# Layer 0 of a two-layer kernel: where the group sums, the spread of the values and the scalings of the last inverse stand

## The chip, the cores and the metric

The kernel runs on one core of one Trainium2 chip. The core has five engines that run side by side, [...]: TensorE (PE in the profile, its weight loads PEld), VectorE (DVE), ScalarE (ACT), GpSimd (POOL) and SyncE (SP), which here only issues DMAs. The metric is the device time of one whole execution in microseconds (us); lower is better. All data is float32.

## The reference, cut to what matters

The input is x, 4 batches of 32 images of 128 x 128 (in the code B = 4, T = 32, and an image's rows and columns are H = C = 128). Layer 0 is a Fourier attention block:

```python
xn = inorm(gn(x))                            # group norm, then per-image norm
k, q, v = (fno(xn, w, s) for w, s in ...)    # spectral convolutions, 32 heads
p = softmax(einsum('bntk,bnsk->bnts', q, k)) # 32 x 32 per head and batch
a = inorm(fno(einsum('bnts,bnsk->bntk', p, v)) + gn(x))
m = inorm1(spectral1(gelu(inorm0(spectral0(inorm(a))) + skip))) ...
x = x + inorm(m) + a
```

Spectral convolutions are products of the low Fourier modes (64 x 33 per image) with weights, so the kernel computes with modes: forward transforms as matmuls with cosines and sines, products in mode space, inverse transforms as matmuls again. Layer 1 (an attention over 1024 tokens per row block and a mixture of experts) follows and takes what layer 0 wrote; it is not changed.

## The kernel before, in words

`layer0` runs over the four batches b. A batch has these stages:

- **The products with the values** (`for x0 in range(0, KX, NK)`, L936 on): modes of the images are broadcast from DRAM into `xb` (L941, four buffers), copied into PSUM as `xw` (L950), multiplied with the value weights `gb` into `u`, most of them on VectorE (L963) and some on GpSimd (L959), and contracted on TensorE with the attention probabilities `pr` into `po` (L898, helper `product`).
- **Inverse transform, the statistics, the spectrum and gelu** (`inverse`, `stats`, `spectra`, `inverse_of`, `gelu`).
- **The boundary to the next batch**, which overlaps the end of batch b with the attention of batch b + 1: `image_scales` (group norm of the next batch), `spectra(1, ...)` (second spectrum of this batch), `spectra_of_images` (modes of the next batch), `coefficients` (the factors c2, c3, cq of the last normalisation), `attention_weights` (scores, softmax, probabilities through DRAM as `prd` and `pr`), and the last inverse of this batch, `back`, which adds its result into `xr` and stores it.

Most of layer 0 is placed by a scheduler that works with estimated times; `behind(later, earlier)` forces an order without a wait. The order that results is fixed in the program. Each engine then takes its queue in order: an instruction that waits holds everything behind it.

Places that the change touches:

- `image_scales` (L438): VectorE makes `both`, TensorE sums it over the partitions (`bg`, L380, in `sums`), and VectorE copies it to `by_group` (L448), all ahead of `colg` and `sv`. `by_group` is read only much later, in `turn` (L914).
- `value_weights` (L604): VectorE makes the weights `g`, one row per head and quarter of the modes. Two DMAs write them to DRAM as `gd` (L620), four DMAs read them back into `gb` (L625), each repeating 16 heads' rows over 8 groups of partitions. It runs once, ahead of batch 0.
- `attention_weights` (L637): `pa` and `pb` (L675, L677), the score matmuls `sp` and `sp0` (L690, L692), `spt` and `spt0` (L695, L700), `sc` (L705 to L715), `mx`, `less`, the exponential `ex` (L722), `sm`, and `ph` (L732, two halves on GpSimd). Its three hooks put work of batch b between: the scalings `g` (L1283, 32 ACT instructions: 16 ahead of `spt`, 8 ahead of `ex`, 8 after it) and GpSimd's additions into x (L1293, four).
- `back` (L359 `four`, L343 `y` in `row_products`, L357 copies `v`) with `last` (L1331): four VectorE instructions per group, each scaling one image by its c3 and adding it. `skip_matrix` (L764 `cm`, L768 `cd`, L769 `cp`) makes the skip weights of the next batch.
- PSUM tags: `wide` has two buffers, shared by `xp`, `y`, `xw` and the sums; `a` and `b` have two each. In SBUF the tag `v` has three.

Of the kernel before, what the change touches and what calls it, by code (L numbers as in the profile page):

```python
# [7 lines left out]
F32 = mybir.dt.float32  # L8
# [122 lines left out]
def layer0(  # L131
# [201 lines left out]

    def row_products(spec, a, ahead=()):


        wide = [ps.tile([P, 2, 512], F32, name="y1", tag="wide") for _ in range(2)]
        for slot in range(4):
            c = slice(slot * P, slot * P + P)
            for k, trig in enumerate((cos_back, sin_back)):  # L340
                for g in range(4):
                    r = slice(32 * g, 32 * g + 32)
                    mm = nc.tensor.matmul(  # L343
                        wide[g // 2][:, g % 2, c],
                        spec[r, 4 * a + slot, 64 - 64 * k : 192 - 64 * k],
                        trig[r],
                        start=k == 0,
                        stop=k == 1,
                    )
                    for earlier in ahead:  # L350
                        behind(mm, earlier)
        return wide
# [7 lines left out]

    def back(spec, a, take, ahead=(), copy=None, apart=False):

        wide = row_products(spec, a, ahead)
        for g in range(4):
            four, inverted, _ = four_images(
                wide,
                g,
                copy or evacuate,
                dict(tag="pr", bufs=6) if apart and a else dict(tag="v", bufs=3),
                "a" if apart and g % 2 else "b",  # L370
            )
            take([image(a, g, k) for k in range(4)], four)
        return inverted
# [64 lines left out]
    def image_scales(sv, gm, gv, shift):  # L438

        gr, _ = inv_std("gn_r", gv, 1)  # L440
        gs = one("gs")
        nc.vector.tensor_mul(gs, gm, gr)

        both = small.tile([P, 2, 32], F32, name="both", tag="both")
        nc.vector.tensor_scalar(both[:, 0], of_group, gr, None, ALU.mult)
        nc.vector.tensor_scalar(both[:, 1], of_group, gs, -1.0, ALU.mult, ALU.mult)
        by_group = small.tile([P, 2, 32], F32, name="by_group", tag="by_group")
        nc.vector.tensor_copy(by_group, sums("bg", ones, both, "a"))  # L448
        colg = small.tile([P, NX], F32, name="colg", tag="colg")
        nc.vector.tensor_scalar(colg, cols, gr, None, ALU.mult)  # L450
        gs128 = one("gs128")
        nc.vector.tensor_scalar(gs128, gs, 128.0, None, ALU.mult)
        gg = one("gg")
        nc.vector.tensor_mul(gg, gs, gs128)
        gr2 = one("gr2")
        nc.vector.tensor_mul(gr2, gr, gr)
        grs = one("grs")
        nc.vector.tensor_scalar(grs, gs, gr, -2.0, ALU.mult, ALU.mult)
        nc.vector.tensor_scalar(sv[:, 1], sv[:, 1], gr2, gg, ALU.mult, ALU.add)
        nc.vector.scalar_tensor_tensor(sv[:, 1], sv[:, 0], grs, sv[:, 1], ALU.mult, ALU.add)  # L460
        nc.vector.tensor_scalar(sv[:, 0], sv[:, 0], gr, gs128, ALU.mult, ALU.subtract)
        sv_op = nc.vector.tensor_scalar(sv, sv, 1.0 / NPIX, None, ALU.mult)
        return by_group, colg, shift, sv, sv_op

# [16 lines left out]
    def spectra_of_images(b, xt, normed, then=None):  # L481


        _, colg, shift, sv, _ = normed
        n = 1 + KY
# [96 lines left out]
        for g in GROUPS:  # L582
            z = grp.tile([P, GI, 2, 32], F32, name="z", tag="z")
            made = half_rows([xt[:, g + t] for t in range(GI)], z, z32[:, :, g : g + GI])
            if g == 0:
                ysc, scaled = image_weights(sv, made)
            if g == GI and then is not None:
                then(made)
# [8 lines left out]
        unfold(1)  # L597
        return xx, (xe, xm), xd, edges, ysc

    def value_weights():  # L600
# [8 lines left out]
        behind(nc.vector.tensor_scalar(p1, pw[:, :, :KA, 0], hv[:, 3:4], None, ALU.add), normed[4])  # L609
        gd = dram.tile([2, NH, NM], F32, name="gd")  # L610
        for ri, (b, d, op) in enumerate(
            ((v_re, v_im, ALU.subtract), (v_im, v_re, ALU.add))
        ):
            g = prep.tile([P, KX // 4, KY], F32, name=f"g{ri}")
            behind(nc.vector.tensor_scalar(g, pw[:, :, :, ri], hv[:, 2:3], None, ALU.mult), normed[4])
# [3 lines left out]
            nc.vector.tensor_tensor(g[:, :, :KA], g[:, :, :KA], t1, ALU.add)  # L619
            written = nc.sync.dma_start(  # L620
                out=gd[ri].rearrange("n (q m) -> (n q) m", q=4), in_=g.rearrange("p x y -> p (x y)")
            )
        for ri in range(2):
            for k in range(2):
                read = nc.sync.dma_start(  # L625
                    out=gb[:, k, ri],
                    in_=gd[ri, 16 * k : 16 * k + 16].unsqueeze(0).to_broadcast([8, 16, NM]),
                )
                if ri == 0:
                    behind(read, written)  # L630

# [3 lines left out]
    def attention_weights(b, front, hooks=None):  # L635

        xx, (xe, xm), _, (x32, w32), _ = front  # L637
        xs = per_image("xs")
# [57 lines left out]
        if ahead is not None:  # L696
            behind(act, ahead)
        ahead = hooks[1](act) if hooks else None
        spt0 = small.tile([2 * NH, T], F32, name="spt0", tag="ym")
# [14 lines left out]
        for o, i in halves:  # L714
            nc.tensor.matmul(o[:, :, 0], both_plus[: 2 * NH], spt0[:, i], start=False, stop=True)  # L715

        mx = small.tile([2 * NH, half], F32, name="mx", tag="mx")
        nc.vector.tensor_reduce(mx, sc, AX.X, ALU.max)
        less = grp.tile(nn, F32, name="less", tag="v", bufs=3)
        nc.vector.tensor_tensor(less, sc, mx.unsqueeze(2).to_broadcast(nn), ALU.subtract)  # L720
        ex = grp.tile([2 * NH, half, 2, T], F32, name="ex", tag="pr", bufs=6)
        softmax = nc.scalar.activation(ex, less.unsqueeze(2).to_broadcast([2 * NH, half, 2, T]), AF.Exp)  # L722
        if ahead is not None:
            behind(softmax, ahead[0])
        sm = small.tile([2 * NH, half], F32, name="sm", tag="mx")
# [3 lines left out]
        for h in range(2):  # L729
            r = slice(32 * h, 32 * h + 32)  # L730
            first = ex.rearrange("n t r d -> n (t r d)")[r, T - half * h :]
            product = nc.gpsimd.tensor_tensor(  # L732
                ph[r],
# [3 lines left out]
            )  # L737
            if ahead is not None:
                behind(product, ahead[1])
        if hooks:  # L740
# [58 lines left out]
    front = spectra_of_images(0, loaded, normed)  # L799
    value_weights()  # L800

# [37 lines left out]
    big, late = (p.__enter__() for p in (pools[-1], right[-1]))  # L839
    weights = attention_weights(0, front)  # L840
    bd = skip_matrix(weights[2], front[4])

# [41 lines left out]
    for b in range(B):  # L884
        xt = loaded
        by_group = normed[0]
        xd = front[2]
# [46 lines left out]
        for x0 in range(0, KX, NK):  # L934
# [3 lines left out]
            for i in range(4):  # L938
                xb = late.tile([P, 2, NK * KY], F32, name="xb", tag="xb")[:, :, :m]
                for r in range(2):  # L940
# [5 lines left out]
                        .to_broadcast([8, 16, m]),  # L946
                    )
                xw = ps.tile([P, 2, 512], F32, name="xw", tag="wide")[:, :, :m]
                for r in range(2):
                    c = nc.scalar.copy(xw[:, r], xb[:, r])  # L950
                    if x0 == 0:
                        behind(c, weights[4])
                for k in range(2):
# [99 lines left out]
        def negative(spec, slots):  # L1053

            nc.scalar.activation(spec[:, slots, :64], spec[:, slots, P:], AF.Copy, scale=-1.0)

# [221 lines left out]
        c2, c3, cq = (made[n] for n in ("c2", "c3", "cq"))  # L1278
        negative(spec, slice(0, GI))

# [14 lines left out]
        images_of = [slice(g, g + GI) for g in GROUPS]  # L1295
        if b + 1 < B:
            def first_half(copied, on_pool):

                for t in range(T // 2):
                    act = scale(t)  # L1300
                    behind(act, copied)
                for i in images_of[:2]:
                    behind(add_scaled(i), on_pool)
                return act

            def third_quarter(scores):

                for t in range(T // 2, 3 * T // 4):
                    act = scale(t)
                    behind(act, scores)  # L1310
                return act, add_scaled(images_of[2])

            def rest(softmax, product):

                for t in range(3 * T // 4, T):
                    behind(scale(t), softmax)
                roots["added"] = add_scaled(images_of[3])
                behind(roots["added"], product)

            weights = attention_weights(b + 1, front, (first_half, third_quarter, rest))  # L1320
        else:
# [4 lines left out]
        for a in HALVES:  # L1326
            groups = [slice(16 * a + g, 16 * a + g + GI) for g in (0, GI)]

            def last(images, four):
                for j, t in enumerate(images):  # L1330
                    nc.vector.scalar_tensor_tensor(  # L1331
                        xr[:, t], four[:, j], c3[:, t : t + 1], xr[:, t], ALU.mult, ALU.add
                    )

# [12 lines left out]
            if b + 1 < B:  # L1347
                inverted = back(spec, a, last, weights[1:2] if a == 0 else (), nc.scalar.copy)
            else:
# [646 lines left out]
```

## Time and profile before

| | us |
|---|---|
| median of 3 runs | 2974.37 (2972.92 to 2975.74) |
| the profiled execution | 2975.87 |
| its span in the profile | 2974.2 |
| batch 0 until its first `po` matmul | 88.28 |
| `po` stages of batches 1, 2, 3 begin | 293.02, 498.14 and 702.91 (a period of 205) |
| layer 1's score loop begins | 887.36 |

| engine | busy us | share of the span |
|---|---|---|
| PE | 2741.9 | 92% |
| DVE | 2189.5 | 74% |
| ACT | 2314.2 | 78% |
| POOL | 2031.1 | 68% |

The span runs from the first instruction to the last; the profiled execution's own time lies 1.67 us above it, and 1.50 us above the median of the runs. The shares are means over stages with different limits: layer 1 takes some 2087 us of the span, so the page's totals say little of layer 0. For layer 0 the chain of waits, the timeline of each engine, and the busy time in chosen stretches are read.

### The profile page before, as it was taken

The numbers are of one execution on the slowest core, as the hardware profiler recorded it, in microseconds if no ns is written. First come the engines' busy times: TensorE is split into PE (matmuls) and PEld (weight loads), VectorE is DVE, ScalarE is ACT, GpSimd is POOL, SyncE is SP. The second block draws the span as 40 slices with busy tenths as digits, with TensorE's granted clock in tenths as the row PEclk, the third lists the DMA queues.
The fourth block names the chain that finished last, engine by engine and source line by source line (L and its number), as shares of the span: only waits on it lengthen the run. The fifth ranks groups of instructions, "written<-read, shape, count | busy, mean of one in ns | idle before, by whom it ended". The sixth has DMA issues, their size and how long they took to land.

```text
span 2974.2 us, 52576 instructions
## 1 busy us (share of the span) xinstructions
PE 2741.9 (92%) x19442; PEld 1356.0 (46%) x19442; DVE 2189.5 (74%) x4934; ACT 2314.2 (78%) x3217; POOL 2031.1 (68%) x1801
## 2 busy tenths in 40 slices
PE   7798988988878999999899999999999999999997
PEld 4365564664644443343444343444444443444443
DVE  4876787788766677775678688666778766877877
ACT  2554555456358999899999999989999998999992
POOL 1703605417308897878987878898787889798773
PEclk7899999999989999999999999999999999999998
DMA  5503304205011101002010100111010020100000
GB/s 127 157 1 66 121 1 103 84 7 149 18 51 43 33 1 40 8 11 62 1 26 15 26 15 8 36 29 33 15 26 15 8 58 13 28 12 22 15 15 15
DMA packets 151985, 112.58 MB, mean 38 GB/s; under 512 B 36366, under 2 KB 140081, under 8 KB 151217
## 3 DMA queue, kind: packets, MB, share of 16 engines
q1 hardware_dynamic: 148465, 107.13, 14.1%
q8 instruction: 154, 2.52, 0.4%
q10 hardware_dynamic: 3264, 2.10, 0.2%
q14 instruction: 102, 0.84, 0.1%
HBM read 68.19 MB, written 20.04 MB: 30 GB/s over the span
## 4 chain that ended last, share of the span: by engine, by line
PE 60%; POOL 13%; ACT 11%; DVE 9%; issue 6%; DMA 1%; SPq 0%; POOLq 0%; DVEq 0%; ACTq 0%
PE d L1786 20%; PE po L1805 12%; PE px L1692 6%; ACT r L1836 5%; PE n L1786 4%; POOL e L1845 3%; POOL e L1844 3%; PE po L898 3%; POOL u L959 2%; ACT e L1852 2%; PE pz L305 2%; POOL kx L1451 2%; DVE r L1841 1%; PE px L1093 1%; DVE xc L1696 1%
## 5 line engine op out<-in xcount | busy, mean ns | idle before, releaser
L1841 DVE TENSOR_TENSOR r<-n,r 128x1024 f32<-128x1024 f32 (+1 forms) x1056 | 962.0, 953 | 479.9 <-PE n L1786 397.9
L1844 POOL TENSOR_TENSOR e<-r 128x512 f32<-128x512 f32 x528 | 674.1, 1277 | 270.7 <-DVE r L1841 270.3
L1836 ACT ACTIVATE r<-d 128x1024 f32<-128x1024 f32 (+1 forms) x1056 | 793.3, 803 | 65.3 <-PE n L1786 57.3
L1848 ACT ACTIVATE r<-r 128x1536 f32<-128x1536 f32 x528 | 784.1, 1485 | 16.8
L1845 POOL TENSOR_TENSOR e<-e,r 128x512 f32<-128x512 f32 x528 | 672.0, 1273 | 41.4
L1786 PE MATMUL d<-qe,ke 32*128 32x512 f32 (+3 forms) x2304 | 606.9, 603 | 39.9 <-ACT r L1836 36.0
L1805 PE MATMUL po<-e,kx 128*128 128x512 f32 (+3 forms) x1152 | 594.9, 605 | 16.0 <-POOL e L1857 16.0
L1786 PE MATMUL n<-qe,ke 32*128 32x512 f32 (+3 forms) x2304 | 606.8, 602 | 0.0
L1786 PE MATMUL n<-qf,kf 32*128 32x512 f32 (+3 forms) x2304 | 554.0, 555 | 0.0
L1786 PE MATMUL d<-qf,kf 32*128 32x512 f32 (+3 forms) x2304 | 552.8, 556 | 0.0
L1696 DVE SCALAR_TENSOR_TENSOR xc<-px,wgt,xc 128x128 f32<-128x128 f32 x1024 | 358.3, 350 | 40.8 <-PE px L1692 9.7
L1852 ACT ACTIVATE e<-e 128x512 f32<-128x512 f32 x528 | 326.4, 618 | 67.3 <-POOL e L1845 66.3
L1805 PEld LDWEIGHTS po<-e,kx 128*128 128x128 f32 x1152 | 176.0, 188 | 394.7 <-issue 309.3
L1786 PEld LDWEIGHTS d<-qe,ke 32*128 32x128 f32 x2304 | 176.6, 183 | 359.2 <-ACT r L1836 339.1
L1786 PEld LDWEIGHTS d<-qf,kf 32*128 32x128 f32 x2304 | 220.7, 186 | 176.2 <-issue 163.8
L1692 PE MATMUL px<-we,x2t 128*128 128x512 f32 x512 | 264.3, 602 | 6.4 <-DVE xc L1696 5.3
L959 POOL TENSOR_TENSOR u<-xb,gb 128x858 f32<-128x858 f32 (+1 forms) x112 | 221.3, 2026 | 65.2 <-PE po L898 48.9
L1786 PEld LDWEIGHTS n<-qf,kf 32*128 32x128 f32 x2304 | 228.5, 186 | 19.5 <-issue 11.5
L1110 POOL TENSOR_TENSOR spec<-part,part 128x512 f32<-128x512 f32 x16 | 25.3, 1580 | 305.8 <-DVE part L1107 111.0
L963 DVE TENSOR_TENSOR u<-xw,gb 128x858 f32<-128x858 f32 (+1 forms) x208 | 216.6, 1111 | 17.6 <-ACT xw L950 13.3
L898 PE MATMUL po<-u,pr 128*32 128x429 f32 (+1 forms) x1280 | 149.4, 531 | 40.4 <-POOL u L959 35.8
L1786 PEld LDWEIGHTS n<-qe,ke 32*128 32x128 f32 x2304 | 177.5, 183 | 10.7 <-DVE r L1841 2.2
(417 smaller groups left out, 3365.8 us busy)
## 6 DMA issues: line engine op xcount, KB each, us to landing
xb<-xd SPq DMA_DIRECT2D x128, 214.5 KB
xc<-x SPq DMA_DIRECT2D x29, 512.0 KB
x<-x SPq DMA_DIRECT2D x16, 512.0 KB
qf<-qe SPq DMA_DIRECT2D x64, 128.0 KB
out<-xc SPq DMA_DIRECT2D x15, 512.0 KB
x<-in_x SPq DMA_DIRECT2D x14, 512.0 KB
xb<-xd SPq DMA_DIRECT2D x32, 198.0 KB
gb<-gd SPq DMA_DIRECT2D x4, 1056.0 KB
```

Of the source, the lines that this page charges most:

```text
L898: mm = nc.tensor.matmul(*args, **kw)
L959: weighed = nc.gpsimd.tensor_tensor(u, xb, gk, ALU.mult)
L1692: nc.tensor.matmul(px, x2t[:, k * P : (k + 1) * P], we[:, e0 : e0 + 4], start=True, stop=True)
L1696: nc.vector.scalar_tensor_tensor(xc[:, k], px[:, e], wgt[:, k, e0 + e : e0 + e + 1], xc[:, k], ALU.mult, ALU.add)
L1786: nc.tensor.matmul(o, k, q, start=turn == 0 or g > 0, stop=turn == 1 or g > 0)
L1805: nc.tensor.matmul(sums[c, h][:, q0 : q0 + c1 - c0], kx[:, jb], e[:, c0:c1], start=jb == 0, stop=is_last and q0 > 2 * P, skip_group_check= ...
L1836: nc.scalar.activation(r[:, g], d, AF.Ln, scale=1.0 / DSCALE)
L1841: nc.vector.tensor_tensor(r[:, g], part, r[:, g], ALU.mult)
L1844: nc.gpsimd.tensor_tensor(e, r[:, 1], r[:, 2], ALU.add)
L1845: nc.gpsimd.tensor_tensor(e, e, r[:, 0], ALU.add)
L1848: nc.scalar.activation(r, r, AF.Exp, scale=-1.0)
L1852: nc.scalar.activation(e, e, AF.Exp)
```

## The change

It touches layer 0 alone and has these parts:

1. `both` is made at the end of `image_scales`; its sum `bg` is taken later, among the row transforms of the next images, and ACT copies it to `by_group`. In batch 0 `image_weights` is called at the second group of images.
2. `value_weights` keeps its weights in SBUF. A new function, `spread_values`, repeats the rows over the partitions by matmuls: 16 PSUM tiles of 128 x 528, two matmuls of 128 x 264 each, with a picked identity as weights; ACT copies each tile to `gb`. The six DMAs by way of DRAM are gone.
3. In batches 0 to 2, c3 is gathered per row of `spec` (`of_slot`, `c3s`, on VectorE) and multiplied into `spec` by one GpSimd instruction of 128 x 1024, ahead of the inverse. `last` becomes one addition per group.
4. The scalings: 24 on ACT ahead of `spt`, with the sign flip `negative` after the eighth; the last 8 on VectorE, after the last product of the scores and ahead of `spt0`.
5. The last inverse's first half begins within the attention: half of `y` after the score matmuls, half after `sc`; the first copy `v` stands ahead of `ex`, the other copies right behind it.
6. `ph` is split: its first half on GpSimd, its second on VectorE.
7. The first load of `xb` of the second and later column blocks is ordered behind the read of `pr`; in batches 1 to 3 the first `xw` copies are ordered behind the last copy `v`.

```diff
-    def row_products(spec, a, ahead=()):
+    def row_products(spec, a, ahead=(), slots=range(4), wide=None):
...
-    def back(spec, a, take, ahead=(), copy=None, apart=False):
-        wide = row_products(spec, a, ahead)
+    def back(spec, a, take, begun=(), copy=None, apart=False):
+        wide, *ready = begun or [row_products(spec, a)]
         for g in range(4):
-            four, inverted, _ = four_images(
...
+            four, inverted, roots["v"] = (
+                ready[g] if g < len(ready) else four_images(
...
-        by_group = small.tile([P, 2, 32], F32, name="by_group", tag="by_group")
-        nc.vector.tensor_copy(by_group, sums("bg", ones, both, "a"))
...
-            if g == 0:
+            if g == (GI if b == 0 else 0):
                 ysc, scaled = image_weights(sv, made)
+            if g == 2 * GI:
+                groups = sums("bg", ones, both, "a")
+                behind(summing["bg"], made)
+                nc.scalar.copy(by_group, groups)
...
-            g = prep.tile([P, KX // 4, KY], F32, name=f"g{ri}")
+            g = grp.tile([P, KX // 4, KY], F32, name=f"g{ri}", tag="v", bufs=3)
...
-            written = nc.sync.dma_start(
-                out=gd[ri].rearrange("n (q m) -> (n q) m", q=4), in_=g.rearrange("p x y -> p (x y)")
...
+    def spread_values(of_row):
+        n = KX * KY // 8
+        picked = grp.tile([P, 2, 4, 8, 16], F32, name="picked", tag="z")
+        for k in range(2):
+            nc.scalar.copy(picked[:, k], steps(ident[:, 64 * k :], [1, 4], [0, 8], [4, 16]))
+        for q in range(4):
+            for k in range(2):
+                rows_of = picked[:, k, q].rearrange("p s n -> p (s n)")
+                for ri in range(2):
+                    to = ps.tile([P, 2, 512], F32, name="gw", tag="wide")[:, :, :n]
+                    for h in range(2):
+                        nc.tensor.matmul(
+                            to[:, h], rows_of, of_row[ri][:, n * h : n * h + n], start=True, stop=True
+                        )
+                    nc.scalar.copy(
+                        gb[:, k, ri, 2 * n * q : 2 * n * q + 2 * n].rearrange("p (h m) -> p h m", h=2), to
+                    )
...
+        copy = hooks[3](scored) if hooks else None
         ex = grp.tile([2 * NH, half, 2, T], F32, name="ex", tag="pr", bufs=6)
         softmax = nc.scalar.activation(ex, ...)
+        if hooks:
+            behind(softmax, copy)
...
-            product = nc.gpsimd.tensor_tensor(
+            eng = nc.vector if h else nc.gpsimd
+            made = eng.tensor_tensor(
...
     weights = attention_weights(0, front)
+    spread_values(of_row)
...
+                    if x0 and i == 0:
+                        behind(broadcast, weights[3])
...
-                        behind(c, weights[4])
+                        behind(c, roots["v"] if b else weights[4])
...
-        negative(spec, slice(0, GI))
+        if b + 1 < B:
+            of_slot = grp.tile([P, 4, 2, 4], F32, name="of_slot", tag="of_slot", bufs=1)
+            nc.vector.tensor_tensor(of_slot, block..., c3..., ALU.mult)
+            c3s = small.tile([P, GI], F32, name="c3s", tag="weighed")
+            nc.vector.tensor_reduce(c3s, of_slot.rearrange("p k i g -> p (k i) g"), AX.X, ALU.add)
+            nc.gpsimd.tensor_tensor(
+                spec[:, :, 64:], spec[:, :, 64:], c3s.unsqueeze(2).to_broadcast([P, GI, P]), ALU.mult
+            )
+        else:
+            negative(spec, slice(0, GI))
...
-                for t in range(T // 2):
+                for t in range(3 * T // 4):
                     act = scale(t)
                     behind(act, copied)
+                    if t == GI - 1:
+                        behind(negative(spec, slice(0, GI)), act)
...
-            def third_quarter(scores):
-                for t in range(T // 2, 3 * T // 4):
-                    act = scale(t)
-                    behind(act, scores)
-                return act, add_scaled(images_of[2])
+            def third_quarter(scores, on_vector):
+                for t in range(3 * T // 4, T):
+                    scaled = nc.vector.tensor_scalar(
+                        gl[:, t], gl[:, t], c2[:, t : t + 1], cq[:, t : t + 1], ALU.mult, ALU.add
+                    )
+                    behind(scaled, on_vector)
+                begun.append(row_products(spec, 0, (scores,), range(2)))
+                return add_scaled(images_of[2])
+
+            def begin(scored):
+                row_products(spec, 0, (scored,), range(2, 4), begun[0])
+                begun.append(four_images(begun[0], 0, nc.scalar.copy))
+                return begun[1][2]
...
-                for t in range(3 * T // 4, T):
-                    behind(scale(t), softmax)
...
             def last(images, four):
-                for j, t in enumerate(images):
-                    nc.vector.scalar_tensor_tensor(
-                        xr[:, t], four[:, j], c3[:, t : t + 1], xr[:, t], ALU.mult, ALU.add
-                    )
+                g = images[0] - 16 * a
+                to = xr[:, 16 * a : 16 * a + 16].rearrange("p (k t) c -> p k t c", k=2)[:, :, g : g + 2]
+                nc.vector.tensor_tensor(to, to, four.rearrange("p (k t) c -> p k t c", k=2), ALU.add)
```

## The prediction

> **What bounds the kernel now.** I read the chain of waits first: which work ended last, in order of time (start, length, what).
>
> ```profile
> 71.15 8.66 DMA prd<-ph
> ...
> 84.67 7.30 DMA xb<-xd
> ...
> 273.37 3.17 ACT g L1283 x8
> 277.06 3.78 PE four L359 x4
> 281.58 1.88 PE four L359 x2
> 287.38 1.85 DVE cp L769 x2
> ```
>
> Batch 0 waits for transfers; the boundary waits for ACT scalings and then for slow inverse matmuls. The timeline of batch 0 shows why (idle time before, and its releaser, in brackets):
>
> ```profile
> 52.74 3.01 SPq L625 DMA_DIRECT2D gb<-gd  x3
> 69.58 6.78 SPq L748 DMA_DIRECT2D prd<-ph  x4
> 83.95 0.52 ACT L950 COPY xw<-xb 128x429 f32<-128x429 f32 x1 [17.06 <-DMA xb<-xd]
> 88.28 4.21 PE L898 MATMUL po<-u,pr 128*32 128x429 f32 x24 [15.03 <-POOL u L959]
> ```
>
> The first `xb` is issued only behind `prd` and `pr`, and all of them share the DMA engines with 4.2 MB of `gb`: ACT stood 17 us, TensorE 15. Next, TensorE at the boundary, and busy time in stretches there (length, busy us of PE, PEld, DVE, ACT, POOL, then the granted clock):
>
> ```profile
> 227.92 0.69 PE L380 MATMUL bg<-both,ones 128*128 128x64 f32 x2 [3.48 <-DVE both L446]
> 228.40 3.73 PE L305 MATMUL pz<-cst,g 128*128 128x128 f32 x16
> 234.03 1.83 PE L305 MATMUL pz<-cst,g 128*128 128x128 f32 x14
> ```
>
> ```profile
> 228.00:232.00 4.00, 4.00 (x18) 3.83 (x18) 3.44 (x13) 0.60 (x1) 0.00 (x0) 0.50 0.00 0
> 232.00:238.00 6.00, 5.87 (x69) 4.11 (x69) 1.55 (x3) 1.54 (x3) 0.00 (x0) 1.00 0.00 0
> 277.00:284.00 7.00, 6.94 (x17) 2.68 (x18) 2.76 (x10) 1.56 (x4) 6.92 (x4) 0.56 0.33 38
> ```
>
> A sum that nobody needs soon holds TensorE 3.48 us, after which the same matmuls take 233 ns a record instead of 131, at clock 0.50. The same happens at 277. Last, VectorE beside GpSimd:
>
> ```profile
> 226.10 1.26 POOL L1110 TENSOR_TENSOR spec<-part,part 128x512 f32<-128x512 f32 x1 [31.44 <-DVE gn_r_t L253]
> 226.22 1.16 DVE L255 TENSOR_TENSOR gn_r<-gn_r,gn_r_t 128x1 f32<-128x1 f32 x1
> 799.91 1.26 POOL L1110 TENSOR_TENSOR spec<-part,part 128x512 f32<-128x512 f32 x1 [23.74 <-DVE va L1039]
> 800.36 0.86 DVE L247 TENSOR_SCALAR r_ve<-va 128x32 f32<-128x32 f32 x1
> ```
>
> Two tiny VectorE instructions (elsewhere 0.16 and 0.17 us) last until GpSimd's ends. During GpSimd's 264.01 to 266.23, VectorE instructions that read PSUM keep their 0.72.
>
> [...] from 20 to 40 TensorE was busy 18.32 us of 20 and stayed at 0.51, which I read as thin matmuls (`pz` of 66 columns) not releasing it.
>
> **Batch 0, step by step.** (1) Sums. In the new order `pz` stands ahead of `mg` and needs only its PSUM, free at 18.2 (copies `sv` end 18.23); before, it began at 22.02. Against that `mg` comes four `pz` later (0.35 us on TensorE, and 1.35 us on the group norm, which meets `it` only after sixteen `pz`). TensorE is 3.5 us earlier; but work that ran at full clock after 44.26 moves into the half-clock time, so I take 2.5 for the first `pa` (49.02 to 46.5). (2) Spread. 32 matmuls of 128x264; two 512-wide `four` take 1.98 at 200.27 (four records, 0.43 apart), so one of 264 costs 0.45 and all 14.4 us. Eight stand among the scores, 3.6 us, where TensorE was busy 11.38 of 13.0 (49 to 62): 1.6 is covered, 2.0 delays the scores. `ex` ends 0.5 earlier than its 66.89. After it eight pairs of 0.9 run before `cm`, so the last ends at 74.3, the first `cd` at 75.8. Sixteen ACT copies of 528 columns (0.52 each, from 0.52 for 429 and 0.5 start to start for 512) hide in ACT's 10.03 idle ahead of `spt` and behind `ex`; uncovered, 8.3. (3) Transfers. 2 writes of 264 KB and 4 reads of 1056 KB go; the eight first `xb` are issued behind `xd`, about 50, ahead of `prd`. `ph` ends near 69.8 with its second half on VectorE, waiting for GpSimd's first: 0.8 saved of 1.5. `prd` then takes 2.95 and `pr` follows in 0.8 (as at 276.27 and 280.03); landed at about 75. So the spread, not the transfers, ends last. (4) VectorE, busy 52.38 of 55.40 from 93 to 148.4, paces the rest. Its `u` began at 86.70. Now the first may start at 75.8, with `cp`, `cd`, `cp`, `bd` (3.1 us) inside the stream: as if at 78.9. **Batch 0: -7.8.**
>
> **Each of three boundaries**, in times of batch 0 to 1. (A) Without `bg` TensorE goes on from 223.5 instead of 228.40, and warm: 4.9 of start plus 1.9 for the 16 records (3.73 to 1.83), less 0.4 for `bg` later: row transforms 6.4 earlier. VectorE's coefficient chain follows `ms`, which now stands behind all 32 `pz`: 240.4 instead of 245.48, -5.1. On it come `of_slot` and `c3s`, 0.4 (two 128x32 rows of 0.19): -4.7. Then the new GpSimd multiply, 128x1024 like L1293's 2.35 us, starts as `c3s` ends; VectorE's `cq` (two SBUF inputs) meets it 0.25 later and holds `xm` and the `xe` copies behind it: 2.1. First `pa`: **-2.6**. The ACT copy of `by_group` (0.23) and `negative` (0.63) hide in ACT's 4.25 idle ahead of `spt`: the 16 scalings ended at 264.01, with eight more (0.39 each) and `negative` it is 267.8, and `spt` starts at 268.26; uncovered, each delays the scores by its length.
>
> (B) Counted on the old clock from `pa` at 255.39. Eight VectorE scalings (0.26 start to start, as L1451's 128x128) reach VectorE at 266.71; GpSimd's first addition began at 266.19 and three follow one another, 2.35 each. [...] two scalings fit between the additions and six come after 273.6: done 275.2. Behind them wait `spt0`, so the last `sc` matmuls, at 275.6 instead of 270.68; TensorE idles 5 us and falls to half clock; `y`'s second half (32 records, 2.2) ends 278.1, `v` 278.7, `ex` 279.7 instead of 273.46. What is late next: `sm`, `ph` (283.9), `pr` (landed near 289). Against it the other `v` copies follow `ex` at once instead of 8 scalings (3.17): `four` begins at 278.7, not 277.06, warms up by 281, and VectorE's additions, 4 of 0.26 each, become one of 0.62. `cm` 283.9, `bd` done 288.9 (was 289.77), the three additions behind it 291.2 with the waits for `four`, one more between the `u`: the `u` stream begins as if at 291.85 instead of 294.17: **-2.3**. `pr` has some 2 us to spare.
>
> Sum: -7.8 + 3 x (-2.6 - 2.3) = -22.5, on a span of 2974.2: 2951.7. The profiled execution reads 1.67 more, the median 0.17 more than the span: **2952**. The last batch and layer 1 (PE 1998.5 busy of 2087) only start earlier.
>
> **Rivals.** (R1) [...] the multiply and the scalings aren't held. For: PSUM readers aren't. Against: 0.86 at 800.36. A becomes -4.7, B about -7.5: -7.8 - 36.6, about **2930**. (R2) The boundary is a draw: VectorE's delay passes wholly through `ph` and `pr`, whose spare 2 us are used up by slower landing (`prd` to `pr` took 10.4 us at 69.58 under load); only batch 0 pays: about **2966**. (R3) TensorE's clock, ends slower: thin work keeps it at half. The spread after `ex` then takes 14.4 instead of 7.2 and `cm` 2.4 more; each boundary loses 1.9 in A, and in B `y` and `four` to the end cost another 5. Total 9.6 + 3 x 6.9 = 30 against 22.5: 2982; it decides once three quarters of these stretches are at 0.50. For: 20 to 44. Against: `four` warmed within 7 us at 277, the spread is 264 columns wide. (R4) `pz` starting before the clock falls at 20.4 keeps it up in batch 0: another 8 off, about **2944**. For: it stayed up from 237 to 255 on such matmuls. [...] (R5) The change doesn't do what it says, the spread replacing one wait by an equal one: batch 0 at 0, **2960**.
>
> **How the numbers follow.** Forecast 0.47, R1 0.09, R2 0.12, R3 0.11, R4 0.13, R5 0.08. The forecast's own range, from A 1 to 4.7 and B 0 to 4 a boundary (three alike) and batch 0 5 to 10, is 2942 to 2962. With R2, R4 and R5 inside, 8 in 10 lie in 2936 to 2968; R1 and R3 outside are 0.20. A measurement tells about 0.2%, 6 us: faster (below 2968.4) 0.83, same 0.06 (half of R2), slower 0.11 (R3).
>
> **What would show it.** No `gd`; `xb` landed before `ph`; the first `po` near 77. `bg` without idle time ahead of it and clock 1.0 from 226 to 232. A VectorE `cq` of some 2 us beside the GpSimd multiply; the first scaling of some 2 us and `spt0` some 7 us behind the last `pb`; `four` beginning 2 us later after `pa` but the `u` stream earlier. A period of 200 instead of 205. Wrong if batch 0's `po` starts after 83, if the boundary's period is 203 or more, or if scalings and additions overlap.

## The result, and the profile after

The change makes the kernel slower by a small amount. The median of nine runs is 2986.88 us against 2974.20 of the kernel before on the same chip; the ratio is 1.0040, 95% interval 1.0031 to 1.0049. The forecast was 2952. The new times also lie further apart (2980.8 to 2992.7) than those of before (2971.8 to 2979.1).

The profiled execution took 2986.88, its span is 2985.2, and the mean granted clock of TensorE is 0.964. To see where the time went I cut layer 0 at events that both traces have: the first `py` of a batch (the first matmul of its inverse transform, behind its products with the values), the first `pa` of the next batch's scores, and the next `py`. From `py` to `pa` is the prediction's part A with gelu and the statistics ahead of it, from `pa` to `py` is part B with the products behind it. Three more names are needed: `pz` are the row transforms (one row of the timeline holds several; a "record" is one matmul in the trace), `it` the column transforms behind them, and `em` the first matmuls that make the modes, ahead of `pa`.

| us, after less before | batch 0 | boundary 1 | boundary 2 | boundary 3 | sum |
|---|---|---|---|---|---|
| batch 0, start to first `py` (148.41 before, 144.36 after) | -4.05 | | | | -4.05 |
| `py` to `pa` (before 106.98, 108.44, 108.60; after 111.03, 110.15, 107.65) | | +4.05 | +1.71 | -0.95 | +4.81 |
| `pa` to `py` (before 96.75, 96.69, 96.23; after 99.11, 101.12, 101.24) | | +2.36 | +4.43 | +5.01 | +11.80 |
| forecast | -7.8 | -2.6 and -2.3 | the same | the same | -22.5 |

The sum is +12.56 at the last `py`; layer 1 begins 11.76 later. So all three parts missed, part B by most. The chain of waits of the kernel after shows the new pieces (start, length, what):

```profile
71.38 7.59 PE gw L641 x32
78.97 1.11 PE cm L784 x4
...
236.23 3.68 PE pz L290 x16
...
252.29 1.22 DVE cq L1290
...
267.57 7.74 DVE g L1350 x8
...
278.44 3.79 PE four L358 x4
...
282.98 5.04 DVE ph L750
```

In batch 0 the DMA pieces are gone, and the spread (`gw`) stands ahead of `cm` in their place. At the boundary there are two kinds of new pieces: slow matmuls (230 ns a record at 236, as at half clock), and two VectorE groups that should have been short, `g` and `ph`. Next is TensorE's timeline (start, length, the idle time before and its releaser in brackets), and busy time in stretches, with the same columns as in the prediction, the clock third from the end:

```profile
229.53 1.11 PE L290 MATMUL pz<-cst,x 128*128 128x66 f32 x8 [0.31 <-ACT z L298]
...
232.96 1.11 PE L290 MATMUL pz<-cst,x 128*128 128x66 f32 x8 [0.53 <-ACT z L298]
234.59 1.11 PE L290 MATMUL pz<-cst,x 128*128 128x66 f32 x8 [0.53 <-ACT z L298]
...
236.23 3.68 PE L290 MATMUL pz<-cst,x 128*128 128x66 f32 x16 [0.31 <-ACT z L298]
```

```profile
228.00:232.00 4.00, 3.69 (x33) 3.56 (x33) 4.00 (x7) 1.98 (x8) 1.75 (x1) 1.00 0.00 0
232.00:238.00 6.00, 4.63 (x31) 4.22 (x30) 2.78 (x13) 2.15 (x11) 0.00 (x0) 0.83 0.00 1
238.00:249.00 11.00, 11.00 (x77) 9.83 (x77) 4.50 (x24) 2.78 (x12) 0.00 (x0) 0.50 0.01 1
277.00:284.00 7.00, 6.33 (x24) 2.70 (x21) 3.43 (x6) 3.07 (x5) 2.37 (x2) 0.50 0.00 0
```

TensorE does go on without waiting for `bg` and at full clock, until 236. But it now waits after each row transform for the single ACT copy of the one before, and after 4 us in which it is busy only 72% (1.47 us of 232 to 234, 1.39 of 234 to 236) its clock falls. It then stays at 0.50 for 24 us (to 260), though from 238 to 249 it is busy 11.00 of 11 us. In the kernel before the clock was 1.00 from 232 to 276.

The last view is VectorE beside GpSimd at the boundary, and what TensorE waits for behind the scalings:

```profile
251.57 1.90 POOL L1312 TENSOR_TENSOR spec<-spec,c3s 128x1024 f32<-128x1024 f32 x1 [19.89 <-DVE c3s L1311]
252.14 1.37 DVE L1290 TENSOR_TENSOR cq<-cq,cg 128x32 f32<-128x32 f32 x1
254.30 2.21 POOL L693 TENSOR_TENSOR pb<-xe,xm 128x544 f32<-128x544 f32 x2 [0.84 <-DVE xm L547]
254.46 1.00 DVE L1294 TENSOR_TENSOR cq<-cq,dq 128x32 f32<-128x32 f32 x1
...
266.97 6.98 POOL L1330 TENSOR_TENSOR x<-x,g 128x1024 f32<-128x1024 f32 x3
267.49 7.82 DVE L1350 TENSOR_SCALAR g<-g,c,cq 128x128 f32<-128x128 f32 x8
275.46 0.29 PE L731 MATMUL sc<-spt,cst 64*32 64x16 f32 x4 [4.20 <-DVE spt L716]
...
281.63 1.50 POOL L750 TENSOR_TENSOR ph<-ex,sm 32x512 f32<-32x512 f32 x1 [7.69 <-DVE sm L744]
282.98 5.25 DVE L750 TENSOR_TENSOR ph<-ex,sm 32x512 f32<-32x512 f32 x1
283.10 2.33 POOL L1330 TENSOR_TENSOR x<-x,g 128x1024 f32<-128x1024 f32 x1
285.40 1.98 POOL L982 TENSOR_TENSOR u<-xb,gb 128x858 f32<-128x858 f32 x1
```

The scalings take 7.8 us, as forecast. `spt` stands behind them on VectorE, so TensorE waits 4.20 us for it, and its clock falls at 273.5 (to 287). The second half of `ph`, for which the forecast allowed nothing, takes 5.25: it ends 0.85 behind the end of GpSimd's first `u` (287.38). Behind it on TensorE, in order, stand the second `cm` (from 288.28) and most of the remaining records of `y` (56 of them in one row, from 289.24), so the rest of the last inverse is late too. At the first boundary TensorE itself waits only 0.33 us for `ph`, since it is still at work at half clock; at the other two it waits 2.31 and 2.37.

### The profile page after: what moved, and what is told of

Its sections match the earlier page's. It is cut to its first block, busy times and chain, and to the rows that moved or that the text cites. A ratio compares the mean times of both kernels' runs of the same rounds, so it can differ in the third digit from the quotient of the medians.

```text
span 2985.2 us, 52645 instructions
## 1 busy us (share of the span) xinstructions
PE 2782.6 (93%) x19506; PEld 1386.5 (46%) x19506; DVE 2220.1 (74%) x4892; ACT 2314.2 (78%) x3215; POOL 2030.6 (68%) x1800
## 4 chain that ended last, share of the span: by engine, by line
PE 60%; POOL 13%; ACT 11%; DVE 10%; issue 6%; DMA 0%; POOLq 0%; DVEq 0%; ACTq 0%
PE d L1833 20%; PE po L1852 11%; PE px L1739 6%; ACT r L1883 5%; PE n L1833 4%; POOL e L1892 3%; PE po L919 3%; POOL e L1891 3%; POOL u L982 2%; ACT e L1899 2%; DVE r L1888 2%; POOL x L1498 1%; DVE xc L1743 1%; PE pz L290 1%; POOL kx L1498 1%
```

## The experiments

All of them are edits of the changed kernel, and each ratio is to the kernel before on the same chip. The theories at the start: A is lost by the late sum itself (L) or by the clock (T), B by VectorE instructions held beside GpSimd's, that is, lasting until those have ended (P), or by the clock (C); for the multiply M, for batch 0 S and W came later.

**e1: the sums early again.**

```diff
-            if g == 2 * GI:
+            if g == 2 * GI and b == 0:
                 groups = sums("bg", ones, both, "a")
...
+        if early:    # in image_scales, at the three boundaries
+            nc.vector.tensor_copy(both, sums("bg", ones, both_scales(), "a"))
```

> The changed kernel, with the group sums (bg) and their VectorE copy back where the kernel before has them, at the three boundaries only. Theory L (the late sum does the harm of stretch A: it takes one of the two PSUM buffers of the row transforms, its ACT copy stands ahead of n_r, TensorE waits for single copies from 229 to 236 and its clock falls): gelu to first pa goes from 50.1 back to about 47 (46.0 before plus 1 for cq held by the new GpSimd multiply), clock 1.0 from 232 to 276; time 2987 - 3 x 3 = about 2978. Rival T (thin row transforms behind ACT copies lose the clock by themselves, and the GpSimd multiply holds the rest): no shorter than 49.5; time 2985 or more.

Measured: 2985.42, ratio 1.0031 (1.0017 to 1.0045). `py` to `pa` is 110.92, 107.07 and 109.34, on average 1.10 longer than before; the changed kernel is 1.60 longer. So putting the sum back gains half a microsecond a boundary, not three, although the clock is 1.00 from the first `pz` to `em` at all three boundaries, as theory L wanted. Busy time in stretches of e1:

```profile
231.00:238.00 7.00, 6.56 (x68) 5.54 (x66) 4.19 (x9) 3.17 (x10) 1.27 (x1) 1.00 0.01 2
238.00:249.00 11.00, 9.96 (x113) 8.96 (x111) 6.36 (x34) 5.14 (x24) 0.00 (x0) 1.00 0.01 1
```

With the early sum the row transforms begin 7 us later (233.05, with its batch 0 ending 0.83 earlier) but run at full clock, and `em` comes only 1.7, 1.0 and 1.5 us later after `py` than in the changed kernel. The head start of the late sum and the slow clock nearly cancel. What e1 still loses to the kernel before lies behind `em`: to `pa` it takes 9.50, 7.16 and 9.50, against 6.69, 7.36 and 7.38. Theory L was right about the clock and wrong about the time: the late sum does little harm on balance.

**e2: the sum last.**

```diff
-            if g == 2 * GI:
-                groups = sums("bg", ones, both, "a")
...
         edges = edge_row()
         unfold(1)
+        groups = sums("bg", ones, both, "a")
+        behind(summing["bg"], stds[-1])
+        nc.scalar.copy(by_group, groups)
```

> The changed kernel, with bg and its ACT copy behind the last mode matmuls (behind unfold(1)) instead of behind the sixth row transform, in all batches. Theory L: TensorE still goes on at 223.5, the row transforms use both buffers after my is read, n_r comes 3 us earlier, no cold clock at 236; gelu to first pa 44 to 45 as the prediction's part A wanted (46.0 less 2.6 is 43.4); time about 2987 - 3 x 5.5 = 2970. Rival T: the waits for single ACT copies stay, clock 0.50 from 236 to 258; time 2984 or more.

Measured: 2985.29, ratio 1.0022 (1.0012 to 1.0032). `py` to `pa` is 108.63, 104.83 and 108.45. In the middle boundary the clock was 1.00 up to `em`, and that one is 3.6 shorter than before; in the other two it fell as in the changed kernel (from the first `pz` to `em` 0.79 and 0.78, there 0.78, 0.75 and 0.77). `pa` to `py` grew to 101.3, 103.4 and 103.9, with the clock at 0.57 to 0.66 between `ph` and the first VectorE `u`. So with the sum out of the way the clock can still fall. That is nearer to rival T, but it isn't yet a test of it.

**e3: the last eight scalings on ACT.**

```diff
                 for t in range(3 * T // 4, T):
-                    scaled = nc.vector.tensor_scalar(
-                        gl[:, t], gl[:, t], c2[:, t : t + 1], cq[:, t : t + 1], ALU.mult, ALU.add
-                    )
-                    behind(scaled, on_vector)
+                    behind(scale(t), act)    # act is the copy spt
```

> The changed kernel, with the last eight scalings on ACT between spt and the exponential instead of on VectorE. Theory P [...]: VectorE's 7.8 us at 267.5 go, last sc matmuls 4.5 us earlier, ex about 4 earlier, u stream 3 to 4 earlier at each boundary; time about 2987 - 3 x 3.5 = 2976. Rival C (TensorE's half clock sets B): the clock still falls in TensorE's idle time at 272, y and four take as long, and the gain is under 1 a boundary; time 2984 or more.

Measured: 2973.15, ratio 0.9982 (0.9968 to 0.9997). `spt` to `ex` falls from 9.52, 9.49 and 9.26 to 4.47 in all three, and `pa` to `py` from a sum of 301.5 to 288.8: 12.7 us, 4.2 a boundary. Theory P holds.

**e4: both halves of `ph` on GpSimd.**

```diff
-            eng = nc.vector if h else nc.gpsimd
+            eng = nc.gpsimd
```

> The changed kernel, with both halves of ph on GpSimd as before. Theory P: the VectorE half of ph takes 5.25 us [...]; with both on GpSimd (2 x 1.5) ph is done 3.5 us earlier at each boundary, batch 0 loses 0.7; time about 2987 - 10 + 0.7 = 2978. Rival C: four, cold, holds cm and the additions anyway; ph done earlier is hidden, time 2985 or more.

Measured: 2978.30, ratio 1.0005 (0.9998 to 1.0011). `ex` to the end of `ph` falls from 9.9 to 6.4 at every boundary, and `pa` to `py` by 9.7 in sum: 1.4 at the first boundary, where TensorE hardly waited for `ph`, and 4.4 and 3.9 at the others. Theory P holds here too.

**e5: the multiply of the modes later.**

```diff
-            nc.gpsimd.tensor_tensor(
-                spec[:, :, 64:], spec[:, :, 64:], c3s.unsqueeze(2).to_broadcast([P, GI, P]), ALU.mult
-            )
...
+            if hooks and yy == 1:
+                hooks[4](on_pool)    # the same multiply, behind the second pb
```

> The changed kernel, with GpSimd's multiply of the modes (c3s into spec) moved behind its first two pb products, where GpSimd waits 4.9 us for TensorE anyhow. Theory M (the multiply holds VectorE's cq and with it the first pa): the cq of 1.37 and 1.00 us become 0.2, first pa 2 us earlier after em at each boundary; time about 2987 - 3 x 2 = 2981. Rival T (cold TensorE and the ACT copy xp set pa): em to pa stays at 9 to 11; time 2986 or more.

Measured: 2992.39, ratio 1.0046 (1.0029 to 1.0063). `em` to `pa` is 10.08, 8.49 and 10.07, where the changed kernel has 11.29, 11.29 and 9.29. In the first and third boundary TensorE was at 0.50 throughout that stretch. The whole run isn't shorter. With the clock moving about, this didn't settle the multiply; e12 does.

**e6: e3 and e4 together.**

> The changed kernel with both edits of e3 and e4: the last eight scalings on ACT, both halves of ph on GpSimd. Theory P [...]: gains add, pa to py falls from 100.5 to about 93 (before 96.6); time about 2987 - 13.7 - 8.6 = 2965. Rival A (the two hide each other, since cm, the second half of y and the pr transfer wait for the same ph): no more than the larger, about 2973.

Measured: 2960.87, ratio 0.9940 (0.9917 to 0.9964). `pa` to `py` is 91.19, 91.95 and 92.19. The gains more than add up (9.7 and 12.7 alone, 26.1 together), so the two don't hide each other, and the kernel is faster than both it started from. GpSimd's timeline, and busy time in stretches that hold the end of the scores, the exponential and the last inverse:

```profile
275.99 3.10 POOL L750 TENSOR_TENSOR ph<-ex,sm 32x512 f32<-32x512 f32 x2 [1.99 <-DVE sm L744]
279.16 2.35 POOL L1329 TENSOR_TENSOR x<-x,g 128x1024 f32<-128x1024 f32 x1
```

```profile
266.00:279.00 13.00, 11.79 (x108) 5.08 (x104) 6.41 (x12) 8.60 (x19) 10.93 (x6) 1.00 0.29 100
279.00:288.00 9.00, 6.70 (x73) 3.61 (x72) 7.75 (x10) 3.92 (x8) 6.36 (x4) 1.00 0.64 147
```

The edits move work of VectorE, ACT and GpSimd only, and TensorE's clock is 1.00 here, where it was 0.50 in the changed kernel; from `spt` to the first VectorE `u` it is 1.00 at all three boundaries, while with e3 or e4 alone it still falls in that stretch at every one. So in part B the slow clock followed from the held scalings and the held `ph`, which leave TensorE idle (4.20 us for `spt` at the first boundary of the changed kernel, 2.31 and 2.37 us for `ph` at the others).

**e7: TensorE filled between the row transforms.**

```diff
+            if fill is not None:    # boundaries only, first three groups of images
+                for j in range(2):
+                    extra = nc.tensor.matmul(fill[:, j], rows, images[k + j], start=True, stop=True)
+                    behind(extra, mm)
             nc.scalar.copy(z[:, k : k + 4], pz[:, :, :, :32])
```

> The changed kernel, with two extra 128x128 matmuls behind each of the first six row transforms of every boundary, into a PSUM tile that nobody reads, so that TensorE doesn't stand still between them. Theory T (the clock falls at 236 because TensorE waits for single ACT copies from 229 to 236, and all that follows at half rate costs A): clock 1.0 from 226 to 254, pz to em 14 to 15 us instead of 18.3, first pa 3 to 4 earlier; time about 2987 - 3 x 3.5 = 2976. Rival V (VectorE's coefficients and the multiply set pa): pa no earlier, time 2986 or more; and if the clock falls all the same, thin matmuls and not the gaps are the cause.

Measured: 2978.29, ratio 0.9998 (0.9985 to 1.0012). TensorE's timeline, and busy time in stretches:

```profile
231.81 1.11 PE L290 MATMUL pz<-cst,x 128*128 128x66 f32 x8
232.76 0.66 PE L299 MATMUL fill<-x,cst 128*128 128x128 f32 x4
233.25 0.34 PE L507 MATMUL it<-colg,z 128*128 128x68 f32 x2
```

```profile
234.00:240.00 6.00, 6.00 (x55) 6.00 (x55) 3.10 (x16) 2.78 (x12) 0.00 (x0) 1.00 0.01 4
240.00:251.00 11.00, 8.27 (x118) 6.73 (x117) 8.67 (x42) 3.78 (x15) 2.20 (x2) 0.99 0.19 26
```

The waits for `z` are filled, the clock stays at 1.00 through the same thin row transforms, and `pz` to `em` takes 14.9 us in each boundary instead of 18.2 to 18.6. `py` to `pa` is 104.85, 103.72 and 103.61, on average 3.95 less than before, and 5.6 less than in the changed kernel. So theory T holds: what the changed kernel loses in part A is the clock, and the extra matmuls, which compute nothing that is used, hold it. It isn't one lucky trace: of the seven traces with the late sum and without them (the changed kernel, e2 to e6, e8), the clock fell between `pz` and `em` at 20 of 21 boundaries; in the five with them (e7, e9 to e12) it was 1.00 there at all 15. What this doesn't separate is the gaps from the width: the extra matmuls are 128 columns wide, so they fill the waits and also make TensorE's work less thin. That the same thin row transforms ran at 1.00 in e1, with few waits (busy 6.56 of 7 and 9.96 of 11 us), speaks for the gaps. The whole kernel gains less than part A, since `pa` to `py` was 7.3 longer in sum than in the changed kernel; the held instructions of part B are still there (7.85 us for the scalings and 5.48 for `ph` at the first boundary), and the clock was at 0.56 to 0.66 between `ph` and `u`.

**e8: the spread of the values in two parts.**

```diff
-    spread_values(of_row)
+    spread_values(of_row, picked, range(2))
     bd = skip_matrix(weights[2], front[4])
+    spread_values(of_row, picked, range(2, 4), roots["cm"])    # behind the last cm
```

> The changed kernel, with the spreading of the values cut in two: the first two of four column groups where they are, the last two behind cm. Theory S (batch 0 falls short because all 32 spread matmuls, most of them after the scores, stand ahead of cm on TensorE): cm at about 75.5 instead of 78.9, cd, cp and bd ahead of the u stream instead of inside it, first py at about 141 instead of 144.4, time about 2987 - 3 = 2984. Rival W (the late first pa, 49.4 instead of 46.5, is the whole shortfall, and u waits for xw, which waits for the gb copies): py 144 or later, time 2987.

Measured: 2987.91, ratio 1.0047 (1.0027 to 1.0066). In the profiled execution TensorE's clock happened to hold in batch 0, with the first `pa` at 40.18 (49.41 in the changed kernel's trace) and the first `py` at 134.61. Nothing ahead of `pa` was edited, so this is the clock (e10, at 1.00 from 20 to 34, has its `pa` at 38.93). From `pa` to `py` it takes 94.43, against 94.95 in the changed kernel: `cm` is 4.6 earlier after `pa`, and the end isn't. That speaks for rival W, though the two traces differ in their clock ahead of `pa`.

**e9, e10: the edits together, then with batch 0 filled as well.** e9 has the edits of e3, e4 and e7. In e10 the extra matmuls are also in batch 0:

```diff
-            if g == 0 and b:
+            if g == 0:
                 fill = ps.tile([P, 2, C], F32, name="fill", tag="wide")
```

> The changed kernel with the edits of e3, e4 and e7 together: scalings on ACT, ph on GpSimd, TensorE filled at the boundaries. Theory (A is the clock, [...] and the two are independent): previous py to first pa 104 as in e7, pa to py 92 as in e6; e6's 2961 less 3 x 4.5 = about 2947. Rival (the clock only moves: warm in A, it falls in B): pa to py back to 96 or more, time 2958 or more.

> As e9, and the same extra matmuls in batch 0 too. Theory (in batch 0 the clock falls at about 22, and everything to 49 at half rate makes the first pa late): pa at about 41 as in e8's profile, where the clock happened to hold, instead of 49.4, first py about 136 to 138; time 8 less than e9's. Rival (what VectorE has to do first, the weights of keys and queries, holds pa): pa at 46 or later, time within 3 of e9's.

Measured: e9 2947.30, ratio 0.9895 (0.9880 to 0.9909), with `py` to `pa` 104.80, 103.78 and 103.60 and `pa` to `py` 91.11, 91.21 and 93.35. Parts A and B are independent, as the theory has it. e10 2935.04, ratio 0.9863 (0.9840 to 0.9885), the fastest of all. Its first `pa` is at 38.93 and its first `py` at 135.28. One stretch of batch 0, in the changed kernel and in e10:

```profile
20.00:34.00 14.00, 14.00 (x91) 13.47 (x91) 7.54 (x42) 4.19 (x20) 0.00 (x0) 0.53 0.00 1
```

```profile
20.00:34.00 14.00, 14.00 (x150) 13.41 (x149) 10.12 (x56) 7.70 (x30) 0.00 (x0) 1.00 0.01 2
```

Both are busy all the time, and one does 150 records (the extra matmuls among them) where the other does 91. Three of e10's four runs are at 2933.7 to 2935.9 with a mean clock of 0.986, one at 2947.3 with 0.981, as in e9, whose trace has batch 0 at half clock (0.50 from 22 to 52). So a batch 0 that keeps its clock is worth some 12 us. That the filling is what keeps it isn't shown: e8's trace kept it without the filling, and the traces of e11 and e12, which have it, lost it at 20 (0.50 from 22 on). One stretch of e11's batch 0:

```profile
28.00:31.00 3.00, 3.00 (x16) 3.00 (x16) 1.87 (x9) 0.39 (x1) 0.00 (x0) 0.50 0.00 0
```

Nor does the filling bring a lost clock back: in e11 TensorE was busy 14.00 of 14 us from 20 to 34, with extra matmuls among its work, at 0.50. By mean clock 6 of the 12 runs of e10 to e12 kept it in batch 0.

**e11, e12: the split spread and the late multiply on top.**

> As e10, and the spreading of the values split as in e8. Theory S: with TensorE at full clock the 32 spread matmuls still stand ahead of cm; splitting them brings cm 2 to 3 earlier and takes cd, cp and bd out of the u stream: first py 1 to 3 earlier than e10's. Rival W (u waits for the xw copies, behind the gb copies on ACT): first py within 0.7 of e10's, as the comparison of e8's and the changed kernel's pa to py (94.4 and 95.0) has it.

> As e11, and GpSimd's multiply of the modes moved as in e5. Theory M: with TensorE at full clock nothing else lies between em and the first pa, and the 8.5 of e7 become 7 (6.7 to 7.4 before); time 4 less than e11's. Rival T: the ACT copy xp or pb holds pa, as in e5; less than 1.5 in all.

Measured: e11 2948.88, ratio 0.9892 (0.9871 to 0.9913); e12 2943.21, ratio 0.9875 (0.9847 to 0.9903). Both profiled executions had batch 0 at half clock (0.50 from 22 on; first `py` at 149.16 and 149.41), so the first `py` can't be compared with e10's. By mean clock: e11's one run at 0.985 took 2938.2 and its three at 0.978 to 0.980 took 2948.2 to 2950.3, 1 to 4.5 above e10's runs of like clock. e9's trace, also at half clock in batch 0 and with its first `pa` at 51.08 (e11: 51.22), has its first `py` at 145.80, so the split loses some 3 us there. It gains nothing. In e12, `em` to `pa` is 6.72, 6.84 and 6.84 instead of e11's 8.41, 8.54 and 8.54, but `pa` to `spt` grew by 0.8 to 1.1, and from `py` to `py` the three boundaries change by -0.8, -0.5 and +1.3. VectorE and GpSimd in e11, then in e12:

```profile
251.21 1.90 POOL L1320 TENSOR_TENSOR spec<-spec,c3s 128x1024 f32<-128x1024 f32 x1 [14.61 <-DVE cq L1298]
251.22 1.93 DVE L1299 TENSOR_SCALAR cq<-cq,par 128x32 f32<-128x32 f32 x1
```

```profile
255.06 1.90 POOL L1346 TENSOR_TENSOR spec<-spec,c3s 128x1024 f32<-128x1024 f32 x1
255.12 1.87 DVE L560 COPY xx<-par 1x16 f32<-1x16 f32 x1
```

The multiply holds the small VectorE instruction that comes beside it: a `cq` of 32 columns in e11 (1.93 us), a copy of 16 elements in e12 (1.87). Moved, it holds the scores instead. Theory M is right about `pa` and wrong about the time: e12's two runs at a mean clock of 0.977 and 0.978 took 2950.6 and 2948.6, as e11's did, and its lower median comes from having two runs of four, not one, at 0.983 or more.

## Why the prediction was wrong, point by point

- **Batch 0, -7.8 forecast, -4.05 measured.** The transfers went off the path as foreseen. Step (1) failed: the first `pa` came at 49.41, not at 46.5. I took TensorE's 3.5 us of head start as worth 2.5, but the kernel before regains its clock at 44.26 and the changed one only past 51, so the whole of it was lost (e8's trace, the same program up to there, kept its clock and has `pa` at 40.18); VectorE then had the weights of keys and queries ahead of `pa` (one, `w_im`, took 1.38 beside GpSimd's `pb`). Step (2) was right in its counting: eight pairs after `ex`, at 0.95 instead of 0.9. But `ex` ended at 70.84, since `pa` was 2.9 late and the way from `pa` to the end of `ex` grew by 3.6, not 2.0. So the last pair ended at 79.0 instead of 74.3, and the first `cd` came at 80.06 instead of 75.8. In step (4) 78.9 became 80.66 with the 4 us of `cp`, `cd` and `bd` inside.
- **Part A, -2.6 forecast, +4.05, +1.71 and -0.95 measured.** The step that failed is "TensorE goes on from 223.5 instead of 228.40, and warm". It was warm to 236 and cold for the next 24 us, while the row transforms, now tied to one ACT copy each, leave TensorE waiting. The step rested on the reading that TensorE loses its clock by one long idle stretch, which the trace of the kernel before shows at 277 (idle for 4.37 us from 272.69, the clock 1.00 to 276.0 and 0.50 from 276.5) but not at 228: there TensorE stood idle from 224.44, and the clock is 1.00 from 224.44 to 225.10 and 0.50 from 225.30 on, so it fell less than 1 us into the wait, behind 2.6 us with TensorE busy 2.04. e7 gives the size: with the clock held, `em` is 3.9, 5.9 and 6.2 earlier than before, against 6.4 forecast for the row transforms, and A is 3.95 shorter. That the multiply holds `cq` was right in kind: 1.37 us where 0.19 is usual, at the first two boundaries. The second held `cq` (1.00 where 0.18 is usual) stands beside GpSimd's first `pb`, which the forecast didn't have; that the two together come to 2.0, against 2.1 forecast, is luck. At the third boundary VectorE makes `c3s` later (673.16), the multiply begins behind the first `pa`, and no `cq` is held: `em` to `pa` is 9.29 there and 11.29 at the other two. With the clock held, the multiply holds one `cq` for 1.93 (e11), and e12 shows that this costs the first `pa` 1.7.
- **Part B, -2.3 forecast, +2.36, +4.43 and +5.01 measured.** The first half was right almost to the digit: the scalings done at 275.31 (275.2; three got through between the additions and five came after, not two and six, which were an estimate), `sc` at 275.46 (275.6), `y`'s half done at 277.8 (278.1), the first `four` at 278.44 (278.7). The step that failed is "`ph` 283.9": it has no wait for VectorE's half, which takes 1.08 in batch 0, while at a boundary GpSimd goes on at once with its last addition and a `u`. `ph` ended at 288.23, 4.3 later than the step has it, and 3.9 and 3.5 later at the other two. The `cm` and the rest of `y` are queued behind it; at the second and third boundary TensorE waited 2.31 and 2.37 us for it, and its clock was at 0.66 from there to the `u` stream, which cost another 2.4 each (10.08 against 7.66). A smaller miss: "warms up by 281" was 287.1, 8.7 us behind the first `four` instead of 2.3 (some 4.5 at the other two). And the eight scalings on VectorE, whose cost the step had right, don't earn it: back on ACT in e3, they give 4.2 a boundary.
- **The rivals.** R3, the one that ended slower, named the clock and a size close to what came (2982). That the size came near is in part luck, for it put the slow clock in the wrong places: batch 0's spread ran at 1.00 (66 to 80), and in part B the held scalings and `ph` were the cause and the clock their consequence (1.00 without them in e6). Of its terms only the one in A holds, with 5.6 us instead of 1.9 by e7. R1 (nothing is held; eight scalings took 7.8 us), R2 (a draw at the boundary, where 4.1 to 6.4 were lost each time) and R5 (batch 0 gained 4.05) fall. R4, a clock that holds in batch 0, didn't come in the trace of the changed kernel, but e8 and e10 show that it is worth 9 to 10 us there (first `py` at 134.61 and 135.28 against 144.36), near the 8 it was given.
- **The marks.** `bg` without idle time ahead of it, the clock at 1.0 from 226 to 232 and the held scalings all came, and no `gd` is left; the held `cq` came at two boundaries of three. The first `po`, to be near 77, was 80.85, and `four` began later after `pa` without an earlier `u` stream. The period of `po` stages, to be 200, was 215.2, 211.6 and 208.3; 203 was the mark for a wrong forecast.

What stays open: which executions of the changed kernel keep the clock where; I have no trace of more than one of them. In part A its boundaries differ by 5 us from each other (+4.05 to -0.95): 2.0 of it is the `cq` that isn't held at the third, 1.6 lies in the kernel before (106.98 against 108.60), and the rest isn't explained. Why TensorE is tied to single copies there is read from its waits, not shown by a run: the small sums `my` and `bg` share the two PSUM buffers of tag `a` with the row transforms, but e2, without `bg` among them, still lost the clock twice. And no run tells whether the waits alone, or the waits together with thin matmuls, make the clock fall.

## What to carry to other kernels

Work moved to an idle engine is not free when its instructions are held beside those of an engine with a long queue: here eight scalings moved to VectorE took 7.8 us beside GpSimd's additions (0.33 is their median), and half of `ph` 5.25 at a boundary (1.08 in batch 0). Look at what GpSimd runs beside and right behind each moved instruction, not only at what it runs now. And an earlier start for TensorE has to be counted with the clock it then runs at; here the same start cost 1.6 us a boundary where the clock fell (the changed kernel) and gained 3.95 where it held (e7). Where short waits for evacuations can't be avoided, matmuls that nobody reads can pay for themselves (e7: ratio 0.9998, against 1.0040 of the changed kernel), put in before the clock falls (in e11's batch 0 they left it at 0.50, with TensorE busy 14.00 of 14 us).

## What the runs showed of the hardware

- In the changed kernel the clock fell behind 4 us with TensorE busy 72% (232 to 236), in which no wait was longer than 0.53 us. So no long idle time was needed. But the busy share alone doesn't decide it. In e6 the clock stayed at 1.00 through a stretch with TensorE busy 1.83 of 3.40 us (283.8 to 287.2, matmuls of 512 columns and a wait of 1.57 us), and in batch 0 of the changed kernel it fell at 20.9 behind 3.15 busy of 3.40 (17.5 to 20.9, mostly matmuls of 8 and 66 columns).
- Once the clock was down, streams of row and column transforms of 66 and 68 columns left it down, at 0.50 and busy 11.00 of 11 us from 238 to 249; so did batch 0's transforms, at 0.53 and busy 14.00 of 14 from 20 to 34. At the boundary it came back at 260 (1.00 from 260 to 272), while the score matmuls ran.
- A held VectorE instruction lasted until one GpSimd instruction had ended, or until two had. Each of the first three scalings got through after one GpSimd addition (8 scalings, 7.8 us beside three additions of 2.3). The `ph` product waited through two GpSimd instructions in a row, 2.33 and 1.98 us, at all three boundaries (5.25, 5.25 and 5.26 us).
